# The last convolution tap goes to SBUF, and silu works there in place

## The chip, the cores and the metric

The kernel runs on one core of a Trainium2 chip. The metric is the device time of one execution in microseconds; the time of a kernel is the median of its runs. The engines are TensorE (PE in the profile, its weight loads PEld), VectorE (DVE), ScalarE (ACT), GpSimd (POOL) and SyncE (SP), which issues all the DMAs of this kernel. On-chip data lies in SBUF or, for what TensorE writes, in PSUM, which is divided into banks of 128 x 512 float32.

## The reference, cut to what matters

Two transformer layers with adaptive layer norm work on x of 16 x 512 x 256 (sequences, tokens, channels). The change lies in the first part of the first layer:

```python
h = layernorm(x) * (1 + ca) + sa
q = l2norm(silu(short_conv(h @ Wq.T, cq)))      # 16 heads of 16
k = l2norm(silu(short_conv(h @ Wk.T, ck)))
v = silu(short_conv(h @ Wv.T, cv))
lr = softplus(h @ Wlr.T + 0.001)
# short_conv: causal, 4 taps, one filter per channel, plus its input
for each chunk of 16 tokens:                     # a scan over 32 chunks
    two fast weights W_in, W_out (4 x 16 a head) give the chunk's output
    and are updated by two inner steps of softmax attention over the chunk
x = x + ga * (norm(o) * gate @ Wo.T)
x = x + gb * low_rank_ffn(...)                   # gelu
# second layer: attention in a window of 64 and four global keys, then a channel mix
```

## The kernel before, in words

**Units.** The work is cut into 16 units (`NU`): 8 blocks of 64 tokens, each for two halves of 8 sequences. `timetable` (L1120) gives each unit u five streams: `prepare` (norm, the projections, the convolutions), `chain` (the scan over the chunks, 4 chunks a unit, in two pieces), `mlp`, `attend` and `mix`. Even units make up one recurrence (half 0) and odd ones the other (half 1); each carries its fast weights from unit to unit. L1129 to L1138 sort all the steps by due time, and the steps of different units are emitted in that order: while unit 12 is prepared, the chains of 9 to 11 run and units 6 to 9 pass through the later layers.

**Order.** The Tile scheduler makes each engine's final instruction list out of this: it takes what is ready by its own cost model, and earlier program order first. Each engine then executes its list strictly in order: an instruction that waits holds all that stand behind it. Buffers of a pool are handed out in program order, and an instruction that writes a new tile waits for the last reader of what was in its place.

**Buffers of the change.** PSUM banks called `bank` come from the pool `ps` with 3 buffers (L103, L111), which is shared by the projections `pp`, the transposes `pt`, the attention's `pq`, `pk`, `pvv`, `pmx`, `tg`, `sg`, `pproj`, and the mlp's and the mix's products. The tile tag `t2k_a` has a ring of 3 SBUF buffers (L118) for, in this order in each unit, `lrT`, six tiles `y`, and two `gsb`; all are stored to DRAM.

**The convolution** (L434 to L474) runs for n = q, k, v and for two channel halves k2. For each, four matmuls (L441) fill a bank `pp`; ACT copies it into `xp`, behind the three last tokens of the block before (L454; POOL moves these, L451 to L456), and scales the bank in place by the tap of the present token plus one (L457); DVE then adds the three older taps, each a `scalar_tensor_tensor` (L459) that reads `xp` and the bank:

```python
for j in range(3):
    ins = nc.vector.scalar_tensor_tensor(
        ppb, xp[:, :, j : j + TB], conv_w[n][:, k2, j : j + 1], ppb, mul, add
    )
```

After both halves, `run` (L220) emits a burst on ACT with high priority: load the table that has Silu, two Silu (L224) from bank to `y`, load the usual table back (L234). The first Silu waits for both convolutions. Four DMAs (L468) then store the two `y`.

**The recurrence's step** (`recur`, L586), named here by its lines: scores `sc_k`, `sc_q`, `sc_v` (L526 multiply, L527 reduce), softmaxes (L538, L540 on DVE, the exponential L541 on ACT, L546 to L548 on DVE, whose last one writes `e_k` or `e_v`), outer products on POOL (L533: `pd_o`, `pd_kv`, `pd_i`), the sum over tokens on DVE (L635: `do`, `di`), a scan on DVE (L630). The two halves go through these side by side.

**Work of other units that stands near the convolutions:** window attention (of units 7 and 8 while 12 is prepared), whose `weigh` (L904) makes `st`, `pT` (L926), `py` and `pz` (L872) and `rs` (L976, L977) and whose result `yT` (L981, DVE) goes into `pproj` (L1003) and `up_c` (L387, DVE) and then into `x` (L389, POOL); the next attention's `pq` and `pk` (L800, L812), evacuated by ACT into `qs` and `keys` (L804, L815).

Of the kernel before, what the change touches and what calls it, by code (L numbers as in the profile page):

```python
# [12 lines left out]
AF = mybir.ActivationFunctionType  # L13
# [4 lines left out]
P = 128  # L18
# [3 lines left out]
TB = 64  # L22
HB = 8
# [72 lines left out]
def adaln_blocks(ctx: ExitStack, tc: tile.TileContext, a: dict, out: bass.AP):  # L96
    nc = tc.nc
    mul, add, sub = ALU.mult, ALU.add, ALU.subtract
# [12 lines left out]
    def bank(name):  # L111
        return ps.tile([P, 512], F32, tag="bank", name=name)
# [7 lines left out]
    def t2k(stream, name, shape=None):  # L120
        return work.tile(shape or [P, 512], F32, tag=f"t2k_{stream}", name=name, bufs=RING[stream])
# [23 lines left out]
    conv_w = []  # L145
# [74 lines left out]
    def run(burst, after):  # L220

        with tc.high_priority():
            for k, args in enumerate(burst):
                ins = nc.scalar.activation(*args[0], **args[1])  # L224
                for dep in after if k == 0 else ():
                    tc.add_manual_dep(
                        ins.ins,
                        dep.ins.name,
                        mybir.DependencyInfo(mybir.DependencyClass.Sync, mybir.DependencyReason.DATA),
                        reason="one load of the table",  # L230
                    )
                if k > 0:
                    tc.keep_in_program_order(ins)
            back = nc.scalar.preload_act_table_set("natural_log_exp_and_others")  # L234
            tc.keep_in_program_order(back)
# [86 lines left out]
    def spill(name, shape):  # L322
        spilled[name] = dram.tile(shape, F32, tag=name, name=name)
        return spilled[name]
# [7 lines left out]
    def hidden(stream, name, cols=TB):  # L332
        t = work.tile([P, 2 * HB * (TB + 1)], F32, tag=f"hT_{stream}", name=name, bufs=1)
        return t[:, : 2 * HB * cols].rearrange("p (k b t) -> p k b t", k=2, b=HB)
# [59 lines left out]
    def place(u):  # L394

        return u % NH, u // NH
# [7 lines left out]
    def load_x(u, name, tag, bufs):  # L404
        x = stage.tile([P, NR, C], F32, tag=tag, name=name, bufs=bufs)
        for e in range(2):
            nc.sync.dma_start(x[e * TB : (e + 1) * TB], rows(a["x"], u, e))
        return x

    def prepare(u):  # L410
        half, tb = place(u)
        b0 = half * HB
        bs = slice(b0, b0 + HB)
        for pc in range(NPC):
            for n in "qkvo":
                spill(f"{n}{u}_{pc}", [HB, H, D, PT])
            spill(f"lr{u}_{pc}", [HB, H, 2, PT])
        x = load_x(u, f"xa{u}", "xa", 1)
        hT = hidden("a", f"hTa{u}")
        yield from norm_T(x, 0, 0, b0, f"a{u}", hT)  # L420
        hf = [hT[:, k].rearrange("p b t -> p (b t)") for k in range(2)]

        pp = bank(f"plr{u}")
        for k in range(2):
            nc.tensor.matmul(pp[: 2 * H, :], lhsT=w_lr[:, k, :], rhs=hf[k], start=k == 0, stop=k == 1)
        lrT = t2k("a", f"lrT{u}", [P, HB, TB])[: 2 * H]
        nc.scalar.copy(lrT.rearrange("p b t -> p (b t)"), pp[: 2 * H, :])
        for pc in range(NPC):
            nc.sync.dma_start(
                spilled[f"lr{u}_{pc}"].rearrange("b h j t -> (h j) b t"),  # L430
                lrT[:, :, pc * PT : (pc + 1) * PT],
            )

        for n in range(3):  # L434
            ys, convs = [], []
            for k2 in range(2):
                tg = tails[:, 2 * n + k2, bs, :]
                tag = f"{u}_{n}_{k2}"
                pp = bank(f"pp{tag}")
                for k in range(2):  # L440
                    nc.tensor.matmul(  # L441
                        pp,
                        lhsT=w_qkv[n][:, k, k2 * P : (k2 + 1) * P],
                        rhs=hf[k],
                        start=k == 0,
                        stop=k == 1,
                    )
                ppb = pp.rearrange("p (b t) -> p b t", b=HB)
                xp = work.tile([P, HB, TB + 3], F32, tag="xp", name=f"xp{tag}", bufs=2)
                if tb == 0:  # L450
                    nc.gpsimd.memset(xp[:, :, 0:3], 0.0)  # L451
                else:
                    nc.gpsimd.tensor_copy(xp[:, :, 0:3], tg)
                nc.scalar.copy(xp[:, :, 3:], ppb)  # L454
                if tb < T // TB - 1:
                    nc.gpsimd.tensor_copy(tg, xp[:, :, TB:])  # L456
                nc.scalar.activation(ppb, ppb, AF.Copy, scale=conv_w[n][:, k2, 3:4])  # L457
                for j in range(3):
                    ins = nc.vector.scalar_tensor_tensor(  # L459
                        ppb, xp[:, :, j : j + TB], conv_w[n][:, k2, j : j + 1], ppb, mul, add  # L460
                    )
                ys.append((t2k("a", f"y{tag}", [P, HB, TB]), ppb))
                convs.append(ins)
                yield
            run([((y, ppb, AF.Silu), {}) for y, ppb in ys], convs)
            for k2, (y, _) in enumerate(ys):
                for pc in range(NPC):
                    nc.sync.dma_start(  # L468
                        spilled[f"{'qkv'[n]}{u}_{pc}"][:, k2 * H // 2 : (k2 + 1) * H // 2].rearrange(
                            "b h d t -> (h d) b t"  # L470
                        ),
                        y[:, :, pc * PT : (pc + 1) * PT],
                    )
            yield  # L474

        gT = spill(f"gT{u}", [P, 2, HB * TB])
        for k2 in range(2):
            pp = bank(f"pgate{u}_{k2}")
            for k in range(2):
                nc.tensor.matmul(  # L480
                    pp, lhsT=w_g[:, k, k2 * P : (k2 + 1) * P], rhs=hf[k], start=k == 0, stop=k == 1
                )
            gsb = t2k("a", f"gsb{u}_{k2}")
            nc.scalar.copy(gsb, pp)
            nc.sync.dma_start(gT[:, k2], gsb)
# [634 lines left out]
    def timetable(u):  # L1120


        yield prepare, [(12, u - 1.7, u - 0.7)]
        yield chain, [(4 * RECUR, u, u + 2)]
        yield mlp, [(10, u + 2, u + 2.65)]
        yield attend, [(2, u + 2.65, u + 2.8), (3, u + 2.95, u + 3.05), (19, u + 3.05, u + 3.95)]
        yield mix, [(8, u + 4.1, u + 4.7)]
# [65 lines left out]
```

## Time and profile before

| | |
|---|---|
| runs | 3237.48, 3243.3, 3245.96 us; median 3243.3 |
| the profiled execution | 3245.84 us, span 3244.0 us, granted TensorE clock 0.823 |
| busy share of the span | PE 75%, PEld 45%, DVE 73%, ACT 54%, POOL 52% |
| DMA queue of the kernel | 23.4% of 16 engines' span, 183.44 MB |
| chain that ended last | DVE 35%, POOL 22%, PE 21%, ACT 10%, issue 8%, DMA 3% |
| third-tap group L459 | 288 instructions, 215.2 us in all, 750 ns each |
| silu L224 to y | 96 instructions, 52.1 us, 594 ns each |
| table loads on ACT | 222, 1283 ns each |

Busy time counts an engine's instructions, not its waits. The wait lists put a wait down to the instruction that ended it. Times on the timelines are microseconds from the start of the span.

### The profile page before, as it was taken

Reading aid. Unit: us, or ns where it says so; the run is one execution under the profiler, and the core shown is the slowest. Engines: PE = TensorE matmul, PEld = TensorE weight load, DVE = VectorE, ACT = ScalarE, POOL = GpSimd, SP = SyncE. Lnnn points to the kernel's source line nnn. Section 1 sums busy time; section 2 is a strip of 40 time slices with the busy share of each in tenths; the row PEclk is TensorE's granted clock in tenths of the full one; section 3 lists DMA queues with packets and bytes.
Section 4 is the critical chain, followed back from the end, with each engine's and each line's share of the span. In section 5 each row is a group of like instructions: output and inputs, shape, how many; then the busy total and the mean of one; then the engine's idle time right before and its main releaser. Section 6 shows DMA issues by size and latency. Waiting matters only on the chain.

```text
span 3244.0 us, 47232 instructions
## 1 busy us (share of the span) xinstructions
PE 2445.9 (75%) x17232; PEld 1472.7 (45%) x17232; DVE 2372.1 (73%) x4513; ACT 1762.4 (54%) x3738; POOL 1677.1 (52%) x1575
## 2 busy tenths in 40 slices
PE   3541156778787778988888888988888888889996
PEld 2110124444444445555455555554545555556564
DVE  1678787878868878878888888878878877873221
ACT  1652354555664656665665656565665545454543
POOL 0245555556656655655646565655556556553112
PEclk8775577878877887988889797989889787879898
DMA  5331112131403223130413122231404121112010
GB/s 150 75 69 20 46 34 70 31 73 39 97 17 77 62 57 76 48 85 21 103 30 94 45 68 65 51 83 34 99 14 105 28 70 37 57 39 59 17 28 27
DMA packets 439307, 186.46 MB, mean 57 GB/s; under 512 B 323937, under 2 KB 413090, under 8 KB 439074
## 3 DMA queue, kind: packets, MB, share of 16 engines
q1 hardware_dynamic: 439074, 183.44, 23.4%
q8 instruction: 135, 2.21, 0.3%
q14 instruction: 98, 0.80, 0.1%
HBM read 116.66 MB, written 66.72 MB: 57 GB/s over the span
## 4 chain that ended last, share of the span: by engine, by line
DVE 35%; POOL 22%; PE 21%; ACT 10%; issue 8%; DMA 3%; SPq 1%; POOLq 0%; DVEq 0%; ACTq 0%
POOL pd_o L533 6%; POOL pd_i L533 5%; DVE pd_kv L630 3%; DVE sc_v L526 3%; DVE pp L459 3%; DVE sv L527 3%; DVE mx L888 2%; DVE do L635 2%; PE st L872 2%; DVE di L635 2%; POOL pd_kv L533 2%; DVE scs L527 2%; PE pQ L742 1%; PE ph L735 1%; PE py L872 1%
## 5 line engine op out<-in xcount | busy, mean ns | idle before, releaser
L533 POOL TENSOR_TENSOR pd_o<-e_k,dt_v 128x1024 f32<-128x1024 f32 x128 | 299.4, 2346 | 242.0 <-DVE e_k L548 242.0
L533 POOL TENSOR_TENSOR pd_i<-e_v,dt_k 128x1024 f32<-128x1024 f32 x128 | 297.3, 2358 | 30.7 <-DVE e_v L548 30.7
L660 POOL TENSOR_TENSOR pd_kv<-hid,pd_kv 128x1024 f32<-128x1024 f32 x64 | 150.5, 2351 | 175.3 <-DVE fw L631 149.3
L872 PE MATMUL st<-qs,keys 32*128 32x128 f32 x2048 | 203.4, 321 | 46.2 <-DVE yT L981 23.3
L635 DVE TENSOR_REDUCE di<-pd_i 128x64 f32<-128x1024 f32 x128 | 155.6, 1216 | 108.6 <-POOL pd_i L533 108.6
L872 PEld LDWEIGHTS st<-qs,keys 32*128 32x128 f32 x2048 | 168.6, 211 | 122.0 <-DVE yT L981 34.3
L872 PE MATMUL sc<-keys,qs 32*128 32x128 f32 x2048 | 167.3, 327 | 74.1 <-DVE yT L981 47.9
L635 DVE TENSOR_REDUCE do<-pd_o 128x64 f32<-128x1024 f32 x126 | 152.9, 1215 | 91.2 <-POOL pd_o L533 91.2
L707 PE MATMUL pwo<-w_WoT,oT 128*128 128x256 f32 x256 | 107.0, 579 | 136.7 <-POOL oT L700 135.9
L872 PEld LDWEIGHTS sc<-keys,qs 32*128 32x128 f32 x2048 | 133.3, 215 | 141.0 <-DVE yT L981 51.2
L888 DVE TENSOR_REDUCE mx<-sc 128x4 f32<-128x512 f32 x256 | 168.0, 682 | 18.5 <-PE sc L869 18.3
L526 DVE TENSOR_TENSOR sc_k<-tok,fw 128x1024 f32<-128x1024 f32 x128 | 155.7, 1216 | 13.8 <-ACT tok L596 12.1
L533 POOL TENSOR_TENSOR pd_kv<-hid,dt_v 128x1024 f32<-128x1024 f32 x64 | 150.5, 2352 | 25.7 <-DVE hid L622 22.7
L630 DVE TENSOR_TENSOR_SCAN pd_kv<-within,pd_kv 128x1024 f32<-128x1024 bf16 x64 | 156.4, 2443 | 0.7
L526 DVE TENSOR_TENSOR sc_v<-tok,fw 128x1024 f32<-128x1024 f32 x128 | 151.0, 1216 | 1.5
L527 DVE TENSOR_REDUCE sv<-sc_v 128x64 f32<-128x1024 f32 x128 | 150.4, 1212 | 0.0
L981 DVE TENSOR_TENSOR yT<-py,rs 128x256 f32<-128x256 f32 x128 | 51.6, 417 | 131.2 <-ACT rs L977 130.8
L735 PE MATMUL ph<-PT,w_v 64*128 64x512 f32 x256 | 119.7, 725 | 34.9 <-ACT z L224 19.8
L707 PEld LDWEIGHTS pwo<-w_WoT,oT 128*128 128x128 f32 x256 | 69.3, 289 | 163.1 <-POOL oT L700 150.3
L1003 PE MATMUL pproj<-w_proj,yT 128*128 128x256 f32 x512 | 129.8, 395 | 17.1 <-DVE yT L981 12.6
L926 ACT ACTIVATE pT<-st 128x512 f32<-128x512 f32 x256 | 133.6, 619 | 15.7 <-PE st L869 15.6
L454 ACT COPY xp<-pp 128x512 f32<-128x512 f32 x96 | 56.6, 589 | 156.8 <-PE pp L441 142.4
(248 smaller groups left out, 7039.2 us busy)
## 6 DMA issues: line engine op xcount, KB each, us to landing
values<-values SPq DMA_DIRECT2D x56, 256.0 KB
gate_a<-gates SPq DMA_DIRECT2D x64, 128.0 KB
xa<-in_x_dram SPq DMA_DIRECT2D x32, 256.0 KB
x<-in_x_dram SPq DMA_DIRECT2D x32, 256.0 KB
gate_c<-gates SPq DMA_DIRECT2D x64, 128.0 KB
gate_d<-gates SPq DMA_DIRECT2D x64, 128.0 KB
q<-y SPq DMA_DIRECT2D x64, 128.0 KB
dt_q<-q SPq DMA_DIRECT2D x32, 256.0 KB
```

The lines of the kernel that those rows point to most:

```text
L526: engine.tensor_tensor(pr, tok.unsqueeze(1).to_broadcast(every), w.unsqueeze(2).to_broadcast(every), mul)
L527: nc.vector.tensor_reduce(dst, pr, AX.X, add)
L533: engine.tensor_tensor(pr, hid.unsqueeze(2).to_broadcast(every), tok.unsqueeze(1).to_broadcast(every), mul)
L630: nc.vector.tensor_tensor_scan(flat, within, flat, 0.0, mul, add)
L635: nc.vector.tensor_reduce(t, pr, AX.X, add)
L660: nc.gpsimd.tensor_tensor(po, qh.unsqueeze(2).to_broadcast([P, R, D, CH]), upto, mul)
L707: nc.tensor.matmul(po[:, n * C : (n + 1) * C], lhsT=pair(oT, k, 2 * b2 + n), rhs=w_o[:, k, :], start=k == 0, stop=k == 1,)
L735: nc.tensor.matmul(ph, lhsT=w_v1[rows, f // 2, :], rhs=pT[rows], start=True, stop=True)
L872: nc.tensor.matmul(dst, lhsT=lhsT, rhs=rhs, start=start, stop=False, skip_group_check=True)
L888: nc.vector.tensor_reduce(mx[:, j], sc[j].rearrange("p (s k) -> p s k", s=NS), AX.X, ALU.max)
L926: nc.scalar.activation(pT[j], st[j], AF.Exp)
L1003: nc.tensor.matmul(po[:, n * C : (n + 1) * C], lhsT=yT[:, k2, par].rearrange("p e t -> p (e t)"), rhs=w_proj[:, k2, par, :], start=k2 == 0 ...
```

## The change

The tile `y` is taken before the taps instead of behind them. Taps 0 and 1 accumulate in the bank as before; tap 2, the last, reads the bank and writes `y` in SBUF. Silu then reads `y` and writes `y`. The bank's last reader is therefore tap 2 on DVE, and no longer Silu on ACT; the first writer of `y` is tap 2, and no longer Silu. The number of instructions of each kind is the same but for the table loads, which the scheduler places.

```diff
                 nc.scalar.activation(ppb, ppb, AF.Copy, scale=conv_w[n][:, k2, 3:4])
+                y = t2k("a", f"y{tag}", [P, HB, TB])
                 for j in range(3):
                     ins = nc.vector.scalar_tensor_tensor(
-                        ppb, xp[:, :, j : j + TB], conv_w[n][:, k2, j : j + 1], ppb, mul, add
-                    )
-                ys.append((t2k("a", f"y{tag}", [P, HB, TB]), ppb))
+                        y if j == 2 else ppb, xp[:, :, j : j + TB], conv_w[n][:, k2, j : j + 1], ppb, mul, add
+                    )
+                ys.append(y)
                 convs.append(ins)
                 yield
-            run([((y, ppb, AF.Silu), {}) for y, ppb in ys], convs)
-            for k2, (y, _) in enumerate(ys):
+            run([((y, y, AF.Silu), {}) for y in ys], convs)
+            for k2, y in enumerate(ys):
```

## The prediction

> **What bounds the kernel now.** I read the page first, then busy time by stretches, the waits, and one steady unit on the timelines of PE, ACT, DVE and POOL.
>
> ```profile
> PE 2445.9 (75%) x17232; PEld 1472.7 (45%) x17232; DVE 2372.1 (73%) x4513; ACT 1762.4 (54%) x3738; POOL 1677.1 (52%) x1575
> ...
> DVE 35%; POOL 22%; PE 21%; ACT 10%; issue 8%; DMA 3%; SPq 1%; POOLq 0%; DVEq 0%; ACTq 0%
> ```
>
> No engine is full, and the chain changes engines all the time. By stretches the middle repeats itself:
>
> ```profile
> 1714.00:1895.00 181.00, 153.93 (x1144) 93.55 (x1142) 148.33 (x283) 110.00 (x234) 104.32 (x99) 0.87 0.26 63
> 1895.00:2076.00 181.00, 153.90 (x1144) 93.56 (x1142) 148.32 (x284) 109.92 (x234) 104.37 (x99) 0.87 0.26 63
> ```
>
> The columns are length, PE, PEld, DVE, ACT, POOL, clock, DMA. A unit takes 181 us; PE is busy for 154 of them, DVE for 148. So a unit's time is made of work plus stalls of in-order queues. Whoever waits for Silu, in the waits of the whole run (us, times, longest):
>
> ```profile
> PE pp L441 <- ACT y L224: 48.2, 8, 10.1
> ...
> PE pq L800 <- ACT y L224: 33.5, 9, 6.3
> ...
> PE pgate L480 <- ACT y L224: 25.8, 3, 11.9
> ```
>
> These are waits for a bank. The 74 us of L441 and L480 lie before 300 us, where PE is busy about 40%; the nine of L800 come about once a steady unit. That place, on PE, ACT, DVE and POOL:
>
> ```profile
> 1931.53 1.88 PE L441 MATMUL pp<-hTa,w_WkT 128*128 128x512 f32 x4
> ...
> 1943.49 3.78 PE L800 MATMUL pq<-hTc,w_w_attnT 128*128 128x512 f32 x4 [4.15 <-ACT y L224]
> ```
> ```profile
> 1942.84 1.08 ACT L224 ACTIVATE y<-pp 128x512 f32<-128x512 f32 x2 [3.43 <-DVE pp L459]
> 1943.94 1.28 ACT L234 ACT_TABLE_LOAD   x1
> 1945.24 0.26 ACT L541 ACTIVATE e_k<-e_k 128x64 f32<-128x64 f32 x1
> ```
> ```profile
> 1928.29 0.35 DVE L548 SCALAR_TENSOR_TENSOR e_v<-e_v,lr,fw 128x128 f32<-128x128 f32 x1
> ...
> 1952.75 0.69 DVE L387 TENSOR_TENSOR up_c<-pproj,gate_c 128x512 f32<-128x512 f32 x1 [1.99 <-PE pproj L1003]
> 1953.36 0.27 DVE L548 SCALAR_TENSOR_TENSOR e_k<-e_k,lr,fw 128x64 f32<-128x64 f32 x1
> ```
> ```profile
> 1950.28 2.34 POOL L533 TENSOR_TENSOR pd_o<-e_k,dt_v 128x1024 f32<-128x1024 f32 x1 [7.14 <-DVE e_k L548]
> 1953.52 1.27 POOL L389 TENSOR_TENSOR x<-x,up_c 128x512 f32<-128x512 f32 x1 [0.90 <-DVE up_c L387]
> 1954.75 2.37 POOL L533 TENSOR_TENSOR pd_o<-e_k,dt_v 128x1024 f32<-128x1024 f32 x1
> ```
>
> PE waits for the bank and then runs at half its rate (3.78 against 1.88 for four); `pproj` behind it is late; DVE stands 1.99 us at `up_c`, and the second recurrence's L548, next in the queue, waits though it has its data; POOL does `x` before that recurrence's `pd_o`. So the attention's delay enters the recurrence.
>
> **The change part by part.**
>
> *Tap 2's duration.* L459 is 750 ns. The nearest row is L1085, one input in PSUM, one in SBUF, output in SBUF: 675. The far end is L1031, all in SBUF, mean 1003 (median 744). So 96 x -0.075 = -7 us on DVE, bounds -7 to +24; I take L1085, whose 32 never exceed 0.69. Half of it may lie on the path: -3.
>
> *Silu from SBUF.* Rows: 594 from PSUM (L224), 640 in place in SBUF (L977): 96 x 0.046 = +4.4 us on ACT. ACT has 71 us idle in each unit; I take 0, and 4.4 if that cover is gone.
>
> *Table loads.* The built program lists 214 where the old one lists 222: a steady unit loses the two around `rs` inside the Gelu burst. The row is 1.28, and `e_k` follows 1.30 behind such a load's start: 8 x 1.3 = -10 us on ACT, bounds 0 (idle time) to -10; taken at 0 beside the walk below. [...]
>
> *The new wait.* Tap 2 must wait for the DMAs out of the ring tile three before, at the head of DVE's queue; behind it would stand the recurrence. In the trace's landing events a store lands 2.8 us (median) after issue, and at the old times tap 2 of (1, 1) starts 16.6 us or more after its slot is free from unit 4 on, the others more; only unit 0 has 2.0. In unit 12 of the new ACT list the first burst stands earlier than before (ahead of four `pT`), so its stores do too, and the slack does not shrink. Cost 0; with no cover it would be a burst plus a store, about 1.1 + 1.3 + 2.8 = 5 us a tap, and that can show in the first units, where bursts follow each other closely (part of the ramp's bound below).
>
> *The bank.* From the copy at L454 to Silu's end a bank is held 14.9 us on average (timelines, 96 cases); to tap 2's end 7.2.
>
> *Ramp, to 300 us.* Banks come sooner, so more taps stand early: 33 instead of 18 in DVE's list before the first scan, 15 x 0.66 = 10 us in front of the first recurrence. Against that, of unit 0's PE waits 7.9 us lie in front of its last Silu. By the end of unit 0 the lists are level. I take 0, bounds -8 to +10.
>
> *The steady unit.* The scheduler picks banks anew and reorders. In the new lists `pq` no longer takes the convolution's bank; `pproj` does, ahead of `py` and `pz`. On DVE both L548 now stand ahead of `up_c`, and on POOL both `pd_o` ahead of `x`. I walk the new DVE list with the old start-to-start times, from the end of the first L548 (1928.64): the two recurrences' four `pd_i` on POOL end at 2.4, 4.7, 7.1 and 9.4 us. The second `di` starts at 7.1 (1.13 us); then two `yT` (0.66), `sk` and its followers (1.5), `di` (1.25), two sums (0.5), `sc_k` (1.13), a tap, `sk`, a tap, L538, and tap 2 of the first half ends at 16.5. Then L540, `di`, L652, L546 and L547 (2.2), a tap, and L548 ends at 19.6; two taps and three small ones bring the second L548 to 21.7. The two `pd_o` so start at 19.7 and 22.1; in the old trace at 1950.28 and 1954.75, that is 21.6 and 26.1. The recurrences gain 1.9 and 4.0, 3 on average.
>
> What is late next: `pproj` starts at 16.5, behind it 3.8 us of `py`/`pz`, `rs`, then `yT`, the second `pproj` and `up_c` at about 28.5, where the old one was at 24.1. Both `do` stand around it on DVE, at about 30 and 32.5, against 31.1 and 35.6 before (1959.72, 1964.27). So 1 to 3 us last here. I take 2.5 a unit, for the 11 units from 5 on: -27.5. Bounds: all 4.0 kept and the stall at L572 (3.47 us, behind the late `qs` on ACT) gone too, -7; or the later `up_c` ruling, +4.
>
> *Sum.* 0 - 27.5 - 3 = -30.5; the profiled execution took 3245.84 (its span and 1.8 around it), so 3215; it stood 2.5 above the median of 3243.3, so **3213**.
>
> **The rivals.**
>
> *The attention becomes the bound (slower).* PE ends `pp` at 1933.4, 4.8 on the walk's clock, and now stands until 16.5: 11.7 us instead of 4.15, with all of `py`, `pz`, `pq`, `pk` behind it and cold. For it: `up_c` comes 4.4 us later in the walk, and each us beyond the old `do` at 31.1 holds both recurrences. Against: `up_c` is one of two a unit, and the recurrences have gained first. It decides when `up_c` ends beyond 31; 3 to 4 us a unit there give 11 x 3.5 = +38, about 3280. [...]
>
> *Hidden.* The bank comes sooner, but the unit stays 181 us since other waits close in: 3243 +/- 10. For it: units from 4 to 9 run through other orders and take 165 to 191 us, mostly 181 to 190, so the order matters little.
>
> *Not what it says.* The bank's release moves with certainty, but if the scheduler uses the freed banks for what waits anyhow, this is the second rival.
>
> **How the numbers follow.** Forecast (the walk holds) 0.57, 3165 to 3233; the attention bound 0.33, 3253 to 3310; hidden 0.10. What a measurement can tell from no change is about 0.3%, 10 us. Faster 0.57, same 0.1, slower 0.33. The range has 0.08 below (all bounds at once) and 0.1 above it: 3160 to 3288.
>
> **What would show it.** Right: tap 2 at 0.68, Silu at 0.64, no wait of PE for `y`, a steady unit of 177 to 180 us, PE waits of `pproj` for L459, `pd_o` waiting less for L548. Wrong: waits of L459 for a DMA, a unit above 182, or DVE's wait at `up_c` or `yT` grown by more than the 27.5 us gained; a ramp moved by over 10.

## The result, and the profile after

The changed kernel takes 3349.57 us (median of four runs, 3344.06 to 3349.73) against 3240.77 for the kernel before (four runs; 3243.3 was the median of the first three): a ratio of 1.032, 95% interval 1.0306 to 1.0334. It is slower by 109 us; forecast was 3213. Lines behind the convolution have numbers one higher than before (L458 and up: L459 is now L460, L630 is L631).

The page of the changed kernel, busy times and the chain that ended last:

```profile
PE 2471.5 (74%) x17232; PEld 1502.5 (45%) x17232; DVE 2411.8 (72%) x4513; ACT 1754.5 (52%) x3730; POOL 1702.4 (51%) x1575
...
DVE 32%; PE 25%; POOL 18%; ACT 12%; issue 8%; DMA 4%; SPq 1%; POOLq 0%; DVEq 0%; ACTq 0%
```

DVE is busy for 40 us more with the same number of instructions, and PE's share of the chain grew from 21 to 25%. Busy time by stretches, an early unit and two late ones (length, PE, PEld, DVE, ACT, POOL, clock, DMA):

```profile
1110.00:1288.00 178.00, 140.34 (x938) 86.85 (x939) 146.46 (x279) 108.28 (x230) 103.29 (x94) 0.82 0.26 64
1859.60:2058.70 199.10, 161.85 (x1155) 99.96 (x1154) 154.57 (x284) 107.10 (x233) 107.85 (x98) 0.80 0.24 57
2058.70:2255.50 196.80, 161.68 (x1136) 98.99 (x1130) 154.28 (x283) 106.96 (x233) 107.86 (x98) 0.80 0.25 58
```

A late unit takes 198 us where it took 181; an early one takes 178. The start times of the scan (L631) of each unit's first chunk show when this happens. The changed kernel is 13.6 us late at unit 0, 4.7 us ahead at unit 2, 10.9 ahead at unit 7 (which starts at 1292.6 us before), then 3.7 late at unit 9 and 93.1 at unit 15. So the loss arises behind some 1300 us. That is where the scheduler's list settles into its repeating form: in units 10 to 13 DVE's list has only about 0.6 of its entries in the same sequence as the old list. This share is called likeness below.

PE's waits for these banks in the whole run (us, times, longest). The waits for Silu (107.5 us at L441, L800 and L480 before) are gone; the bank now comes with the last tap:

```profile
PE pp L441 <- DVE y L460: 17.5, 7, 6.4
...
PE pgate L481 <- DVE y L460: 11.1, 2, 6.7
...
PE pq L801 <- DVE y L460: 6.6, 1, 6.6
```

The new path itself, by line and shape (min/median/max in ns): the last tap into SBUF takes 0.743 us, the other taps 0.750, and Silu in place 0.624 instead of 0.595.

```profile
L460 DVE SCALAR_TENSOR_TENSOR y<-xp,w_ck,pp x32: 730/744/750, 88.9 to 2582.2; 128x512 f32<-128x512 f32 x32
...
L224 ACT ACTIVATE y<-y x96: 612/624/635, 89.0 to 2623.0; 128x512 f32<-128x512 f32 x96
```

The place that the prediction walked, in the new steady list, on DVE's timeline (start, duration, what, and in brackets the wait before it):

```profile
2161.32 0.35 DVE L549 SCALAR_TENSOR_TENSOR e_v<-e_v,lr,fw 128x128 f32<-128x128 f32 x1
...
2177.55 0.75 DVE L460 SCALAR_TENSOR_TENSOR pp<-xp,w_ck,pp 128x512 f32<-128x512 f32 x1 [2.42 <-ACT pp L457]
...
2186.29 0.28 DVE L549 SCALAR_TENSOR_TENSOR e_k<-e_k,lr,fw 128x64 f32<-128x64 f32 x1
2190.25 0.69 DVE L678 TENSOR_REDUCE ov<-osq 128x32 f32<-128x512 f32 x1 [3.67 <-ACT osq L558]
...
2193.35 0.69 DVE L387 TENSOR_TENSOR up_c<-pproj,gate_c 128x512 f32<-128x512 f32 x1 [0.80 <-PE pproj L1004]
```

Both L549 do stand ahead of `up_c`, as the walk had it. But a tap stands in DVE's list ahead of its copy from ACT and waits 2.42 us, because PE made `pp` late, and both recurrences wait behind it. The two `pd_o` on POOL start 23.1 and 25.6 us after the end of the first L549 (2161.67), where the walk had 19.7 and 22.1 and the old trace 21.6 and 26.1; `up_c` starts at 31.7, where the walk had 28.5 and the old trace 24.1.

The largest piece of the loss lies elsewhere, at the Gelu burst, which the walk did not reach: ACT's instructions between the load of the table that has Gelu and the load of the usual one, for the low-rank mlp of another unit. Behind it in ACT's queue stand the exponentials of `hid`, which belong to the recurrence's step (made by DVE at L612). ACT there:

```profile
2090.27 1.28 ACT L224 ACT_TABLE_LOAD   x1
2095.11 1.27 ACT L224 ACTIVATE z<-ph,c_b 128x512 f32<-128x512 f32 x2 [3.56 <-PE ph L736]
2100.39 0.69 ACT L224 ACTIVATE z<-ph,c_b 128x512 f32<-128x512 f32 x1 [4.01 <-PE ph L736]
...
2112.64 1.28 ACT L234 ACT_TABLE_LOAD   x1
...
2115.19 0.65 ACT L978 ACTIVATE rs<-rs 128x512 f32<-128x512 f32 x1
2115.72 0.32 ACT L613 ACTIVATE hid<-hid 128x128 f32<-128x128 f32 x1
2115.92 0.27 ACT L542 ACTIVATE e_k<-e_k 128x64 f32<-128x64 f32 x1
2116.07 0.32 ACT L613 ACTIVATE hid<-hid 128x128 f32<-128x128 f32 x1
```

and DVE beside it:

```profile
2100.63 0.29 DVE L612 TENSOR_TENSOR hid<-scs,fw 128x128 f32<-128x128 f32 x1
...
2106.53 0.29 DVE L612 TENSOR_TENSOR hid<-scs,fw 128x128 f32<-128x128 f32 x1
...
2110.14 1.22 DVE L636 TENSOR_REDUCE do<-pd_o 128x64 f32<-128x1024 f32 x1 [2.45 <-POOL pd_o L534]
2115.88 0.76 DVE L982 TENSOR_TENSOR yT<-py,rs 128x256 f32<-128x256 f32 x2 [4.52 <-ACT rs L978]
```

DVE has made the two `hid` at 2100.9 and 2106.8. Their exponentials stand in ACT's list behind the whole burst and behind `rs`, and run at 2115.7 and 2116.1. The burst of the old list, on ACT:

```profile
1861.92 1.28 ACT L224 ACT_TABLE_LOAD   x1
...
1869.56 0.60 ACT L976 ACTIVATE rs<-pz 128x512 f32<-128x512 f32 x1
...
1877.66 1.28 ACT L234 ACT_TABLE_LOAD   x1
...
1882.34 0.36 ACT L612 ACTIVATE hid<-hid 128x128 f32<-128x128 f32 x1
```

There `rs` stands inside the burst (with two table loads of its own), and the first `hid` is made only after the burst and waits about 2.6 us (made 1879.8, run 1882.34). The loads that a late unit saves in the new list are those that had let `rs` through. The burst itself is longer too: 23.7 us from the first load's start to the last one's end, for 11 of which ACT stands idle for PE, against 17.0 with 1.3 idle. Part of that is PE's rate: behind a gap of 1.92 us it makes four of the burst's products `ph` in 2.08 us, where the old trace has 1.13. First the new list, then the old one (in the unit behind the one just shown):

```profile
2090.30 1.93 PE L873 MATMUL py<-pg,vglob 32*32 32x128 f32 x32 [1.92 <-ACT pg L939]
...
2093.00 2.08 PE L736 MATMUL ph<-PT,w_v 64*128 64x512 f32 x4
```
```profile
2041.26 1.13 PE L735 MATMUL ph<-PT,w_v 64*128 64x512 f32 x4
```

A unit can be cut at three scans, here as means of units 10 to 13. From its first chunk to its second, with the Gelu burst, the old kernel takes 80.5 us; from there to the third chunk, with the place that was walked, 90.5; from there to the first scan of the next unit, 9.6. The changed kernel takes 90.2, 92.7 and 15.0.

### The profile page after: what moved, and what is told of

Read it like the earlier page. It is cut to its first block, busy times and chain, and to the rows that moved or that the text cites. A ratio compares the mean times of both kernels' runs of the same rounds, so it can differ in the third digit from the quotient of the medians.

```text
span 3347.9 us, 47372 instructions
## 1 busy us (share of the span) xinstructions
PE 2471.5 (74%) x17232; PEld 1502.5 (45%) x17232; DVE 2411.8 (72%) x4513; ACT 1754.5 (52%) x3730; POOL 1702.4 (51%) x1575
## 4 chain that ended last, share of the span: by engine, by line
DVE 32%; PE 25%; POOL 18%; ACT 12%; issue 8%; DMA 4%; SPq 1%; POOLq 0%; DVEq 0%; ACTq 0%
POOL pd_i L534 5%; DVE pd_kv L631 4%; POOL pd_o L534 4%; DVE sc_v L527 3%; DVE sv L528 3%; POOL pd_kv L534 3%; PE ph L736 2%; PE py L873 2%; PE pp L441 2%; PE pz L873 2%; PE pproj L1004 2%; PE st L873 2%; DVE pp L460 2%; DVE mx L889 2%; DVE scs L528 2%
## 5 line engine op out<-in xcount | busy, mean ns | idle before, releaser
L534 POOL TENSOR_TENSOR pd_o<-e_k,dt_v 128x1024 f32<-128x1024 f32 x128 | 300.1, 2349 | 207.1 <-DVE e_k L549 207.1
L534 POOL TENSOR_TENSOR pd_i<-e_v,dt_k 128x1024 f32<-128x1024 f32 x128 | 297.0, 2349 | 58.8 <-DVE e_v L549 58.6
L873 PE MATMUL sc<-keys,qs 32*128 32x128 f32 x2048 | 192.1, 325 | 75.0 <-DVE mx L889 62.3
L708 PE MATMUL pwo<-w_WoT,oT 128*128 128x256 f32 x256 | 94.8, 530 | 201.6 <-POOL oT L701 195.8
L873 PE MATMUL st<-qs,keys 32*128 32x128 f32 x2048 | 182.5, 334 | 80.8 <-DVE yT L982 53.8
L661 POOL TENSOR_TENSOR pd_kv<-hid,pd_kv 128x1024 f32<-128x1024 f32 x64 | 150.1, 2346 | 143.2 <-DVE fw L632 100.2
L873 PEld LDWEIGHTS sc<-keys,qs 32*128 32x128 f32 x2048 | 160.0, 216 | 133.7 <-DVE mx L889 76.5
L873 PEld LDWEIGHTS st<-qs,keys 32*128 32x128 f32 x2048 | 153.7, 224 | 134.7 <-DVE yT L982 59.3
L889 DVE TENSOR_REDUCE mx<-sc 128x4 f32<-128x512 f32 x256 | 168.4, 677 | 25.6 <-PE sc L870 25.6
L631 DVE TENSOR_TENSOR_SCAN pd_kv<-within,pd_kv 128x1024 f32<-128x1024 bf16 x64 | 177.2, 2768 | 0.7
L534 POOL TENSOR_TENSOR pd_kv<-hid,dt_v 128x1024 f32<-128x1024 f32 x64 | 152.9, 2389 | 47.3 <-DVE hid L623 42.6
L454 ACT COPY xp<-pp 128x512 f32<-128x512 f32 x96 | 56.7, 591 | 181.0 <-PE pp L441 176.2
L528 DVE TENSOR_REDUCE sv<-sc_v 128x64 f32<-128x1024 f32 x128 | 150.0, 1209 | 0.0
```

What stands on the lines that cost most here:

```text
L528: nc.vector.tensor_reduce(dst, pr, AX.X, add)
L534: engine.tensor_tensor(pr, hid.unsqueeze(2).to_broadcast(every), tok.unsqueeze(1).to_broadcast(every), mul)
L631: nc.vector.tensor_tensor_scan(flat, within, flat, 0.0, mul, add)
L661: nc.gpsimd.tensor_tensor(po, qh.unsqueeze(2).to_broadcast([P, R, D, CH]), upto, mul)
L708: nc.tensor.matmul(po[:, n * C : (n + 1) * C], lhsT=pair(oT, k, 2 * b2 + n), rhs=w_o[:, k, :], start=k == 0, stop=k == 1,)
L873: nc.tensor.matmul(dst, lhsT=lhsT, rhs=rhs, start=start, stop=False, skip_group_check=True)
```

## The experiments

The question was whether the new path costs the time (last tap into SBUF, Silu from SBUF: the path theory), or the other list that the scheduler makes of it (the order theory). The runs combine the path, tile by tile, with whatever list that gives. "Unit" is a quarter of the time from the first scan of unit 10 to that of unit 14, in one profiled run. The number beside a list is its likeness to the list named; e5 stands for the third, e7 for the fourth.

| run | tiles on the new path in late units | DVE's late list | unit, us | median, us | ratio, 95% interval |
|---|---|---|---|---|---|
| before | 0 of 6 | old | 180.6 | 3240.8 to 3245.9 | |
| changed | 6 of 6 | new | 197.8 | 3349.6 | 1.032 (1.0306 to 1.0334) |
| e1_all_but_q0 | 5 | old (0.95) | 181.2 | 3216.8 | 0.9913 (0.9896 to 0.9929) |
| e2_all_but_q1 | 5 | new (1.00) | 195.9 | 3343.1 | 1.0298 (1.028 to 1.0315) |
| e3_q_only | 2 | new (0.96) | 196.7 | 3347.3 | 1.0311 (1.029 to 1.0331) |
| e4_first_eight | 0 (6 up to unit 7) | old (1.00) | 180.2 | 3246.7 | 1.0005 (0.9996 to 1.0015) |
| e5_new_path_bank_held | 6 | third | 202.4 | 3359.9 | 1.0364 (1.0331 to 1.0398) |
| e6_old_path_bank_held | 0 | third (0.96) | 204.7 | 3396.4 | 1.0477 (1.042 to 1.0533) |
| e7_hid_first_new | 6 | fourth | 195.3 | 3340.5 | 1.0304 (1.0263 to 1.0345) |
| e8_hid_first_old | 0 | fourth (0.93) | 193.9 | 3324.4 | 1.0255 (1.0222 to 1.0288) |
| e9_rs_first_new | 6 | another | 194.8 | 3358.9 | 1.0356 (1.0319 to 1.0394) |
| e10_burst_later_new | 6 | near the fourth (0.94) | 191.9 | 3271.6 | 1.0087 (1.0056 to 1.0119) |
| e11_old_other_due | 0 | another | 193.7 | 3335.2 | 1.0284 (1.0255 to 1.0312) |
| e12_first_eight_and_kv | 4 (6 up to unit 7) | old (0.95) | 178.8 | 3218.4 | 0.9926 (0.9903 to 0.9948) |
| e13_k_and_v | 4 | old (0.95) | 179.3 | 3217.2 | 0.991 (0.9895 to 0.9925) |
| e14_kv_and_q1_early | 4 (5 up to unit 7) | old (0.95) | 179.3 | 3218.7 | 0.9927 (0.9908 to 0.9945) |

### Part of the tiles, in either list

One edit serves seven of the runs: a condition on n, k2 and u beside `j == 2`, and Silu reads the bank where it is false. For e1:

```diff
-                        y if j == 2 else ppb, xp[:, :, j : j + TB], ...
+                        y if j == 2 and (n > 0 or k2 == 1) else ppb, xp[:, :, j : j + TB], ...
-                ys.append(y)
+                ys.append((y, y if (n > 0 or k2 == 1) else ppb))
-            run([((y, y, AF.Silu), {}) for y in ys], convs)
+            run([((y, src, AF.Silu), {}) for y, src in ys], convs)
```

The condition is `n > 0 or k2 == 0` in e2, `n == 0` in e3 and `u < 8` in e4.

**e1_all_but_q0.** 

> The change in 80 of the 96 convolution tiles: all but the first half of q (n = 0, k2 = 0), whose last tap stays in PSUM. DVE's list of a late unit then is that of the kernel before (0.95 of its entries in the same sequence, against 0.57 for the changed kernel's). Order theory (the loss is the other order of the queues from about unit 9 on, and the new path itself costs nothing): steady unit 179 to 183 us as before, total 3225 to 3255. Path theory (last tap into SBUF, Silu from SBUF, two engines more on SBUF, cost the time tile by tile): 5/6 of +109, about 3330; steady unit 195.

**e2_all_but_q1.** 

> Again 80 of the 96 tiles, but the one left out is the second half of q (n = 0, k2 = 1). DVE's list of a late unit is the changed kernel's, entry for entry. Order theory: steady unit 196 to 200 us, total 3335 to 3355. Path theory: the same as the run with the first half of q left out, about 3330, and no difference between the two.

**e3_q_only.** 

> The change for q alone, 32 of the 96 tiles. DVE's list of a late unit is the changed kernel's (0.96). Order theory: steady unit 196 to 200 us, total 3330 to 3355 although two thirds of the change are gone. Path theory: a third of +109, about 3277; steady unit 187.

**e4_first_eight.** 

> The change in units 0 to 7, the old path in units 8 to 15. Lists: the changed kernel's up to unit 5, the old kernel's, entry for entry, from unit 10 on. Order theory: the changed first units reach scan (6, 1, 0) 12 us earlier, as in the changed kernel, then 181 us a unit: total 3225 to 3240, below before. Path theory: the first half pays too, only hidden by the ramp: 3245 to 3300.

e1 and e2 have the same number of tiles on the new path, 126 us between their medians, and units of 181.2 and 195.9 us. e3 has a third of the change and all of the loss (22 us of it up to unit 8, the rest in late units of 196.7). The path theory falls with these three, unless the whole cost were to lie in the first half of q; the pairs below and e11 exclude that. A late unit of e1:

```profile
1807.00:1988.00 181.00, 151.79 (x1144) 93.75 (x1145) 150.27 (x285) 109.91 (x236) 104.02 (x98) 0.87 0.27 63
```

Length, clock and the busy times of ACT and POOL are those of before; DVE's is 2 us above it, so five sixths of the new path are there and cost the unit nothing. e1 even beats the kernel before; its total lies below the 3225 to 3255 expected. By its scans it gains 28.8 us up to unit 9 (from unit 3 to 5, 4 to 6 and 5 to 7 a unit takes 172.6 to 174.5 us, against 179.2 to 180.2) and nothing behind. In those units its list is neither the old one (likeness about 0.7 in unit 5) nor the new one (about 0.8).

e4 missed: 3225 to 3240 expected, 3246.7 measured. Its first units were ahead as expected (13.2 us at unit 7), but the change from the new list back to the old one, in units 8 and 9, took it all back: 2.7 ahead at unit 8, 6.4 late at unit 10, then 180.2 a unit.

### The same list with and without the change

In e5 the changed kernel holds each bank until behind Silu; e6 has the same addition and none of the change.

```diff
-            run([((y, y, AF.Silu), {}) for y in ys], convs)
+            run([((y, y, AF.Silu), {}) for y, _ in ys] + [((scr, ppb[:, 0, :1], AF.Silu), {}) for _, ppb in ys], convs)
```

**e5_new_path_bank_held.** 

> The changed kernel, with a Silu of one element per partition out of each PSUM bank behind the two Silus, so that the bank is released as late as before (about 0.2 us of ACT more per tile, the changed kernel's data path). Its lists are a third pattern: round the Gelu burst that of the changed kernel (hid, rs behind the whole burst), elsewhere different (0.82 like the changed kernel, 0.50 like the old one). Order theory: the same steady unit, within 2 us, as the run that follows, which has the old path in nearly the same list (0.96). If the place of the Gelu burst is what costs, 195 to 199 us a unit and a total of 3335 to 3360; if the rest of the list, 180 to 186 and 3240 to 3280. Path theory: 10 us a unit or more above the run that follows.

**e6_old_path_bank_held.** 

> The kernel before, with the same two Silus of one element per burst and nothing of the change. DVE's list of a late unit is like the one of the run with the new path and the bank held (0.96) and not like that of the kernel before (0.50). Order theory: far from 3243 although no part of the change is in it: as slow as its twin, within 2 us a unit. Path theory: a unit of 181 to 183 us (16 tiny activations of 0.2 us on an engine with 70 us idle), total 3240 to 3260.

In e7 and e8 the exponential of `hid` gets the bursts' priority, e7 from the changed kernel, e8 from the one before:

```diff
-        nc.scalar.activation(hid, hid, AF.Exp)
+        with tc.high_priority():
+            nc.scalar.activation(hid, hid, AF.Exp)
```

**e7_hid_first_new.** 

> The changed kernel with the exponential of hid at the priority of the bursts: in ACT's list of a late unit both recurrences' hid now stand inside the Gelu burst (two table loads more for the second) and not behind it and rs. If hid's place behind the Gelu burst is what makes the unit long (in the changed kernel the two recurrences' hid were ready 14.8 and 9.2 us before they ran), the unit falls to 184 to 190 us and the total to 3260 to 3300; if not, 195 to 200 us and 3330 to 3360.

**e8_hid_first_old.** 

> The kernel before with the exponential of hid at the priority of the bursts and nothing of the change. Its ACT list round the Gelu burst is then, entry for entry, that of the changed kernel with the same edit. Order theory: the same steady unit as that kernel, within 2 us, whatever it is. Path theory: 10 us a unit or more below it.

A late unit of e6, which has none of the change:

```profile
1887.40:2092.20 204.80, 164.69 (x1143) 100.20 (x1142) 150.86 (x284) 112.69 (x243) 106.03 (x98) 0.78 0.23 55
```

24 us more a unit for six tiny activations (not 16, as the expectation has it) and two table loads (ACT's busy time +2.8, beside 71 us idle before): the list does this, not the work. In the two pairs the kernel with the new path is 2.3 us a unit faster (202.4 against 204.7; within 2 was expected) and 1.4 slower (195.3 against 193.9). So under nearly the same list the path is worth some 2 us a unit at most, of either sign, against 17. e5's unit lies above both ranges that were expected of it. On `hid` itself, e7 gave back 4.9 us of the 9.7 in the stretch with the Gelu burst (85.3 instead of 90.2), but the next stretch grew to 95.0, and of 17 a unit 2.5 came back: the second of its two answers (195 to 200), well short of 184 to 190.

### What stands behind the Gelu burst, and another due time

```diff
-            nc.scalar.activation(rs, pz, AF.Ln)
-            nc.scalar.activation(rs, rs, AF.Exp, scale=-1.0)
+            with tc.high_priority():
+                nc.scalar.activation(rs, pz, AF.Ln)
+                nc.scalar.activation(rs, rs, AF.Exp, scale=-1.0)
```

**e9_rs_first_new.** 

> The changed kernel with the two activations of rs (ln and exp of the softmax sums) at the priority of the bursts. In ACT's list of a late unit one hid then stands ahead of the Gelu burst and rs inside it, as in the kernel before, instead of both behind it. If what stands behind the Gelu burst makes the unit long (DVE waited 4.5 us for rs there and a recurrence some 10 us for hid), the unit falls to 183 to 190 us and the total to 3250 to 3305; if not, 194 to 200 us and 3320 to 3360.

```diff
-        with tc.high_priority():
+        with ExitStack():
             for f in range(F // P):
                 rows = slice(RANK * (f % 2), RANK * (f % 2 + 1))
                 ph = abank(f"ph{i}_{f}")
```

**e10_burst_later_new.** 

> The changed kernel with the eight matmuls ahead of Gelu at normal priority. ACT's list of a late unit then has rs ahead of the Gelu burst and the first hid inside it. If what stands behind the burst makes the unit long: 183 to 190 us, total 3250 to 3305. If not (DVE's list is still 0.80 that of the changed kernel): 194 to 200 us, 3320 to 3360.

```diff
-        yield prepare, [(12, u - 1.7, u - 0.7)]
+        yield prepare, [(12, u - 1.6, u - 0.6)]
```

**e11_old_other_due.** 

> The kernel before with nothing but the due time of the convolutions' steps moved by a tenth of a unit (1.6 to 0.6 ahead instead of 1.7 to 0.7). Same instructions, another list (0.55 like the old one in a late unit). Order theory: a unit anywhere from 178 to 205 us, a total off the old one by more than 20 us either way. Path theory: 3230 to 3255, as nothing is added or removed.

ACT in e10, at the Gelu burst of a late unit:

```profile
2248.83 0.60 ACT L977 ACTIVATE rs<-pz 128x512 f32<-128x512 f32 x1 [5.59 <-PE pz L873]
...
2250.11 1.28 ACT L224 ACT_TABLE_LOAD   x1
...
2254.72 0.29 ACT L613 ACTIVATE hid<-hid 128x128 f32<-128x128 f32 x1
...
2261.47 1.28 ACT L234 ACT_TABLE_LOAD   x1
...
2265.13 0.34 ACT L613 ACTIVATE hid<-hid 128x128 f32<-128x128 f32 x1
```

`rs` goes ahead, the first `hid` waits 0.1 us (made 2254.6), and the burst takes 12.6 us instead of 23.7 (14.6 in the other three of units 10 to 13). The stretch with the burst falls to 81.8 us: 8.4 of its 9.7 us are back. So most of the loss in this stretch goes with the burst. Its length and what stands behind it are not separated: e10 changes both, while e7 and e9, which move `hid` or `rs` and leave the burst at 21 to 28 us, bring the stretch to 85.3 and 87.6. The unit of e10 gains only 5.9 us, since the next stretch grows to 95.1 and the last stays at 15.0. The 183 to 190 us were missed by 2. e9 brought 194.8 a unit, which is the answer foreseen for the case that what stands behind the burst is not what makes the unit long, and with longer units from 4 to 9 no better total. e11 shows that a tenth of a unit in one due time, with not an instruction added or removed, costs 92 us.

### Back in the old list

The condition is `u < 8 or n > 0` in e12, `n > 0` in e13 and `n > 0 or (k2 == 1 and u < 8)` in e14.

**e12_first_eight_and_kv.** 

> The change in units 0 to 7, and from unit 8 on for k and v alone (q as before). The lists are the changed kernel's up to unit 5 and the old one's from unit 8 on (0.95). Order theory: 12 us ahead at scan (6, 1, 0) as in the changed kernel, then 180 to 182 us a unit, and a shorter change-over than with the old path from unit 8 on, since unit 8 is already 0.95 like the old list: 3215 to 3240. Path theory: 80 of 96 tiles changed, about 3330.

**e13_k_and_v.** 

> The change for k and v in all units, q as before (64 of the 96 tiles). DVE's list is that of the run with all but the first half of q, in every unit from 1 on (0.99 to 1.00), so its units 2 to 8 should bring the same 28 to 30 us. If the steady unit of 178.8 us (run with the first eight units and k, v) against 181.2 (run with all but the first half of q), under the same DVE list, comes from q's second half, this one has 178 to 180 us a unit and a total of 3198 to 3212; if it was chance or the changed first units, 180.5 to 182 and 3213 to 3222. Path theory: 2/3 of +109.

**e14_kv_and_q1_early.** 

> The change for k and v in all units and for the second half of q in units 0 to 7 only. The same DVE list again. If q's second half on the new path costs the late units 2.4 us, this run is as fast late as the one before (178 to 180 us a unit) and 3198 to 3212 in all; if it does not, 3213 to 3222.

The four runs e1, e12, e13 and e14 have the same DVE list from unit 6 on (likeness 0.99 or 1.00) and units of 181.2, 178.8, 179.3 and 179.3 us, on average 1.0 below the old kernel's 180.6. That is little: e4, whose late list is the old one entry for entry, is 0.4 below it, and the four lists differ from the old one in a twentieth of their entries. Of e13 and e14 the late unit was within one of the two answers foreseen (178 to 180), the total within the other (3213 to 3222). That q's second half takes the gain away is not shown: the totals of all four lie within 2 us, with runs of one kernel up to 18 us apart. The unit of e12 lies below the 180 to 182 expected, its total within 3215 to 3240. In e13 the units up to 9 brought 20.6 us and not the 28 to 30 expected. All four are faster than both kernels: by 0.7 to 0.9% than the one before, by 4% than the changed one.

## Why the prediction was wrong

**The failed step is the steady unit**: -2.5 us for each of 11 units was forecast, and the late units came out 17.2 us longer. The walk took the new DVE list at one place, some 35 us of 181, and gave its entries the old start-to-start times, and so the old phase of PE and ACT. There it was right on the order, and wrong on the times, as a tap waited for ACT, `ov` for ACT and `st` on PE for `yT`. The rest of the list, of which about four tenths had changed too, was left out. It carried most of the loss: 9.7 us in the stretch with the Gelu burst and 5.4 between the two recurrences' scans, beside 2.2 in the stretch that holds the walked place, where 2.5 were to be gained. Between the scans DVE stands for POOL: the scan at 2240.30 takes 4.14 us where the old one takes 2.28, and behind it DVE waits 1.00 us for `rs_b` and spends 2.28 on L353.

DVE's ledger over two late units (361.9 us before, 395.9 after) says what kind of time it is. Idle time grew by 21.7 us (65.4 to 87.1). The largest waits, first before, then after (us, times, longest):

```profile
DVE di L635 <- POOL pd_i L533: 14.7, 6, 4.5
DVE do L635 <- POOL pd_o L533: 8.2, 6, 1.4
DVE lr L572 <- ACT lrt L210: 6.9, 2, 3.5
DVE yT L981 <- ACT rs L977: 5.0, 2, 2.5
```
```profile
DVE do L636 <- POOL pd_o L534: 21.3, 8, 3.6
DVE pp L460 <- ACT pp L457: 12.9, 8, 2.9
DVE di L636 <- POOL pd_i L534: 10.9, 6, 2.2
DVE yT L982 <- ACT rs L978: 10.4, 2, 5.8
DVE ov L678 <- ACT osq L558: 7.3, 2, 3.7
```

The wait of `lr` (L572), whose end the bound of -7 had counted in, did shrink, from 6.9 to 1.0 us, and the unit grew all the same. Busy time grew by 12.3 us: eight scans took 7.0 us more, L900 4.7 more, L353 about 3.7 more and L1032 4.3 less, depending on what POOL does beside them (below).

**Where the walked list was kept, the term was too large but near in kind.** In e1 both L549 stand ahead of `up_c`, and PE's `pq` no longer waits for Silu:

```profile
1898.11 0.35 DVE L549 SCALAR_TENSOR_TENSOR e_v<-e_v,lr,fw 128x128 f32<-128x128 f32 x1
...
1920.59 0.28 DVE L549 SCALAR_TENSOR_TENSOR e_k<-e_k,lr,fw 128x64 f32<-128x64 f32 x1
1923.84 0.69 DVE L387 TENSOR_TENSOR up_c<-pproj,gate_c 128x512 f32<-128x512 f32 x1 [2.97 <-PE pproj L1004]
...
1927.49 1.19 DVE L636 TENSOR_REDUCE do<-pd_o 128x64 f32<-128x1024 f32 x1
```

On the walk's clock (from 1898.46) the two `pd_o` start at 21.6 and about 23.9, against 19.7 and 22.1 in the walk and 21.6 and 26.1 before: a gain of 0 and 2.2 instead of 1.9 and 4.0. A unit gained 1.0 us (-0.6 to 1.8 over the four runs with this list) instead of 2.5.

**The small terms.** The last tap's duration was taken from L1085 (675 ns) and is 743: -0.7 us in all instead of -7. L1085 was a poor neighbour; the tap's own row was nearer. Silu was taken at 640 and is 624: +2.8 us on ACT instead of +4.4, in idle time. The table loads are 214 as forecast; counting them as a gain, if a hidden one, missed that they went because `rs` went behind the burst. The new wait for the ring's DMAs was put at 0, and no tap waits for a DMA in the trace. The ramp was put at 0 with bounds of -8 to +10: the first scan came 13.6 us late, outside, but unit 2 was 4.7 ahead, inside.

**The rivals.** The slower one came nearest in the sign, and its point was passed (`up_c` at 31.7, beyond 31), but it was not its mechanism: DVE waits less at `up_c` than before (1.6 us in two units against 4.0), and it was priced at 3 to 4 us a unit. The argument within the second (hidden), that units 4 to 9 run through other orders at 165 to 191 us and so order matters little, was the costly one: by the scans of the old trace those units take 176 to 185 us, and the settled late lists of these runs range from 178.8 to 204.7. The range of 3160 to 3288 had no case for a different settled list.

**What stays open.** Why the lists other than the old one are all long is shown only in part, and for one stretch (e10); the rest would need runs that move one entry and keep all others, and none of the edits here did that. That the old list is an unusually good one fits all fourteen runs, but was not tried by itself.

## What to carry to other kernels

Where a scheduler orders in-order queues, a change that frees a buffer earlier is first of all a new order: compare the settled lists of all engines before pricing anything, and if the steady list differs as a whole, put the spread that other lists show into the range rather than a walk of one place. To price the change itself, apply it to parts of its tiles until one variant falls back into the old list; here that separated an effect of some 1 us a unit from 17 of order, and gave the four fastest kernels, though most of their gain came in the first nine units, from yet other lists. A table load that goes away is read together with what it had let through.

## What the runs showed of the hardware

A DVE scan over 128x1024 takes 2.25 to 2.31 us alone, and also where POOL's small copies (L453, L456) run beside it, but 3.26 to 4.38 where an outer product of POOL (L534) is under way when it starts. This holds for 8 of the 64 scans in the old trace and 18 in the new one, and makes most of the scans' growth from 156.4 to 177.2 us. Where one of POOL's 128x512 instructions (L675, L389) still has 0.9 to 1.0 us to go, it is 3.02 to 3.16. It goes the other way too: two `hlast` copies take 2.32 us beside such a scan, one of them 2.18, and 0.19 each in the old trace. First DVE, then POOL:

```profile
2240.30 4.14 DVE L631 TENSOR_TENSOR_SCAN pd_kv<-within,pd_kv 128x1024 f32<-128x1024 bf16 x1
...
2255.50 2.26 DVE L631 TENSOR_TENSOR_SCAN pd_kv<-within,pd_kv 128x1024 f32<-128x1024 bf16 x1
```
```profile
2239.95 2.34 POOL L534 TENSOR_TENSOR pd_kv<-hid,dt_v 128x1024 f32<-128x1024 f32 x1 [2.00 <-DVE hid L623]
2242.24 2.32 POOL L1027 COPY hlast<-hp 128x8 f32<-128x8 f32 x2
```

L900, with two small inputs in SBUF, goes from 0.17 to as much as 2.37 us in the same way. L353 goes from 0.15 to as much as 2.32 beside L534 and L661, and in the old trace L1031 from 0.71 to 2.88 beside L533. So how long these DVE instructions take depends on the order of POOL's list, which a row's mean from the trace of before does not say. Scan and L900, with two inputs in SBUF, are lengthened by 2.10 and 2.19 us at most, no more than one L534 lasts (median 2.34). L528, with one input, stays at 1.21 beside L534 (36 times). The tap reads one input from SBUF and keeps to 0.717 to 0.750 us with its output in SBUF, 0.723 to 0.781 with it in the bank; eight taps with the new output start while an L534 is under way and take 0.734 to 0.748, so in this trace the new output does not bring the tap into this. The granted clock of TensorE was lower in the long units: 0.86 to 0.89 in late units of 178 to 182 us (before, e1, e12), 0.78 to 0.83 in late units of 191 to 205 (changed, e2, e3, e6, e10). PE stands idle longer there: 27 us of 181.0 before, 35 to 38 of 196.8 to 199.1 in the changed kernel. Inside one list clock and length need not go together: in e3 a unit of 197.4 us has 0.78 and one of 192.6 has 0.83, in e2 one of 196.4 has 0.83 and one of 192.6 has 0.81. The Gelu burst was longer where more of its 16 products `ph` took over 0.8 us each: in units 10 to 13 of the kernel before none in three units, with a burst of 17.0 us, and three in one, with 18.4; in those of the changed kernel 8 in one, with 23.7, and 10 in three, with 25.0. No run here separates how much of a long unit the lower clock makes and how much of the clock follows from it.
